# First image's attention: three key tiles of eight converted by DMA from a ring, folding with three scores of eight, VectorE's other work dealt later

## The chip, the cores and the metric

The kernel runs on one core of a Trainium2 chip. The metric is the device time of one execution in microseconds; the time of a kernel is the median of several runs. The engines are called TensorE (PE, matmuls), VectorE (DVE), ScalarE (ACT), GpSimd (POOL) and SyncE (SP); each works through its own list of instructions in order and waits on semaphores for the others. Transfers are issued from an engine's queue and carried out by the core's 16 DMA engines.

## The reference

Eight images of 512 channels and 32 x 32 = 1024 positions go through two attention layers. The first has eight heads of 64 channels, and fake-quantises q, k and v to 8 bits over the whole batch:

```python
h = group_norm(xf, gn_w, gn_b)
qkv = jnp.einsum('oc,bct->bot', qkv_w, h) + qkv_b[None, :, None]
...
q = fake_quant(q); k = fake_quant(k); v = fake_quant(v)
w = jnp.einsum('bct,bcs->bts', q * scale, k * scale)
w = jax.nn.softmax(w, axis=-1)
a = jnp.einsum('bts,bcs->bct', w, v)
a = jnp.einsum('oc,bct->bot', proj_w, a) + proj_b[None, :, None]
return xf + a
```

The second layer is a group norm and an attention with a single head of 512 channels, again with a projection and a residual. The quantisation needs the smallest and largest values of q, k and v of all images, so no attention can begin before every image's qkv is there.

## The kernel before

**Stages.** First, q, k and v of all eight images are computed and written to DRAM. Then comes the attention of the first image, with nothing of the second layer beside it, since the second layer of an image needs the whole of its first. From then on the attention of image b+1 is woven into the projection and the second layer of image b, step by step; a planner (`InOrder.planned`) with costs and due times deals the work of VectorE and ScalarE there. In the first image's attention the planner is off (`InOrder.planned` is false): `later` runs its work at once, and a hand-made list, `dealt`, takes its place.

**The attention's units.** `attention()` goes over units u = (image, head pair j, query half hf, key tile s): two halves and eight key tiles of 128 keys make 16 units for a pair, 64 for an image. For each unit,

- `scores(u)` issues two matmuls "st" (128 keys x 512 queries, for both heads of the pair) into one of two score banks, and ScalarE's exponential writes them to a float32 tile `pt` of 128 x 1024;
- `split(u)` makes two half-precision parts of it: a cast into `two[:, 0]`, and on VectorE the remainder, `two[:, 1] = pt - two[:, 0]` (a TENSOR_TENSOR, called a subtraction below);
- `over_keys` multiplies both parts with v into the bank "av", and `totals` adds up the rows into "sm" with a matmul against ones.

In the first image key tiles 3 and 7 (`plain`) aren't split: their float32 exponentials stand in a tile "aside" and go into float32 matmuls. PE's order in this stage is: scores of two units some six to eight units ahead, then av and sm of two units, and so on; the scores of tile 7 of a half stand directly ahead of the av of its tiles 0 and 1. The tiles `pt` come from a pool of four buffers, `two` from a pool of six.

**Who casts, before.** Tiles 2 and 6: GpSimd. Tile 5: VectorE (while the planner is off). Tiles 0, 1 and 4: ScalarE. The subtraction of a tile is issued straight after its cast.

**What else runs in this stage.** `fold()` multiplies the second layer's weight matrices with each other: a generator of 35 steps, mostly one float32 matmul of 128 x 512 each, with copies of the results by ScalarE and some sums by VectorE. Nine steps are taken before the attention begins; then each odd unit of the first image takes one (`next(folding, None)` in `scores`). Half-way through it issues the loads of the first image's x (2 x 1 MB, tile h), and at its end it stores four tiles (wm_d). `load_pair` fetches q and k of the next pair from DRAM 16 units ahead, and v once the second buffer `raw` is free; VectorE quantises each in two steps (`quant`, `quant2`; v has a third, `whole`, on a quarter of it for the plain tiles). `finish` ends a half: two copies by ScalarE, and after the second half the row sums go through small DMAs (`apart`, `rs_d`, `rs`) with `spread` (sum and reciprocal) and `divide` on VectorE.

`dealt` holds (unit from which it may run, name, work); `deal(u)`, called once by each `split`, runs the first entry that may run. `settle` runs all entries of a name. Before, for a pair fetched at unit u: q and k from u + 10, v's fetch from u + 10, v's steps from u + 18; spread from u + 10 and divide from u + 17 of the half's last units.

Where a unit's instructions are issued from helpers, the profile gives one line for many: L91 for VectorE's and ScalarE's, L208 for all matmuls, L1047 for GpSimd's casts. On SP, L945 are the fetches of q, k and v, L1129, L1143 and L1145 the transfers of the row sums, L1215 the loads of x, L1768 the stores of wm, L1255 the stores behind the projection.

Of the kernel before, what the change touches and what calls it, by code (L numbers as in the profile page):

```python
# [9 lines left out]
F32 = mybir.dt.float32  # L10
# [8 lines left out]
P = 128  # L19
B, C, HH, WW = 8, 512, 32, 32  # L20
T = HH * WW
CC = C // P
NT = T // P
# [35 lines left out]
def attn_pair_kernel(  # L59
# [246 lines left out]
    with ExitStack() as fast:  # L306
# [611 lines left out]
        def deal(u):  # L918
            i = next((i for i, (at, *_) in enumerate(dealt) if at <= u), None)
            if i is not None:  # L920
                dealt.pop(i)[2]()

        def settle(what):
            while True:
# [4 lines left out]
            dve.settle(what)  # L929

        ao = {}

        def load_pair(b, j, u=None):

            nm = f"{b}_{j}"
            raws = []

            def fetch(i, src):
                if (b, j, i) == (0, 0, 2):
                    raw = aop.tile([P, NH, 512], F32, tag="ao", name="raw_first").rearrange(  # L940
                        "p h n -> p (h n)"
                    )
                else:
                    raw = raw_p.tile([P, T], F32, tag="raw", name=f"raw_{nm}_{i}")
                nc.sync.dma_start(  # L945
                    raw if i < 2 else raw.rearrange("p (t d) -> p t d", t=NT), src
                )
                raws.append(raw)

            def whole(raw, _, i):  # L950
                quant2(raw.rearrange("p (t d) -> p t d", t=NT)[:, 3::4, :], vfs[j], i)

            fetch(0, q_d[b][j])
            fetch(1, k_d[b][j])
            qt = qkp.tile([P, T], BF, tag="q", name=f"q_{nm}")
            kt = qkp.tile([P, T], BF, tag="k", name=f"k_{nm}")
            vt = qkp.tile([P, NT, P], F16, tag="v", name=f"v_{nm}")
            todo = (qt, kt, vt.rearrange("p t d -> p (t d)"))

            if b == 0:  # L960
                vfs[j] = xp.tile([P, 2, 256], F32, tag="x", name=f"vf_{nm}")[:, :, 0:P]

            def quants(i):
                for step in (quant, quant2, *([whole] if i == 2 and b == 0 else [])):
                    name, work = "qk" if i < 2 else "qv", lambda step=step: step(raws[i], todo[i], i)
                    if u is None or InOrder.planned:
                        dve.later(name, 0.7, work, pe.t + 12.0, 45.0)
                    else:
                        dealt.append((u + (10 if i < 2 else 18), name, work))

            def fetch_v():
                if len(raws) == 2:
                    fetch(2, v_d[b][:, :, bass.ts(j, P)])
                quants(2)

            if (b, j) == (0, 0):
                fetch(2, v_d[b][:, :, bass.ts(j, P)])
            quants(0)
            quants(1)
            if u is None or InOrder.planned:  # L980
                dve.later("qk", 0.0, fetch_v)
            else:
                dealt.append((u + 10, "qk", fetch_v))
            return qt, kt, vt


        def attention():

# [4 lines left out]
                     for s in range(NT)]  # L993
            pairs = {}
            pairs[0, 0] = load_pair(0, 0)
            pts, parts, avs, sms, rss, ready = {}, {}, {}, {}, {}, {}
            st_free, at_hand = [0.0, 0.0], set()

            aside = l2p.tile([P, 3, NT // 2, 256], F32, tag="vsum", name="aside")
# [1 line left out]
            def scores(u):  # L1001
                b, j, hf, s = units[u]
                if hf == 0 and s == 0:
                    settle("qk")
                nm = f"{b}_{j}_{hf}"
                qt, kt, _ = pairs[b, j]
                st = pair_ps(f"st_{nm}_{s}")
                if b == 0 and u % 2 == 1:
                    next(folding, None)
                awaits(st_free[-2])  # L1010
                for i, r in enumerate(HALF):
                    mm(
                        st[:, i, :], lhsT=kt[r, bass.ts(s, P)],
                        rhs=qt[r, bass.ts(hf, 512)], start=True, stop=True,
                    )
                if u >= 4:
                    need(u - 4)
                if plain(b, s):
                    pt = aside[:, u // 4 % 3].rearrange("p (i k) n -> p i (k n)", i=2)
                else:  # L1020
                    pt = ptp.tile([P, 2, 512], F32, tag="p", name=f"pt_{nm}_{s}")
                there = act.do(
                    1.12, lambda: act.activation(pt, st, AF.Exp, scale=esc),
                    max(pe.t + 0.25, ready.get(u - 4, 0.0) + 0.1),
                )
                st_free.append(there)
                pts[u] = pt, there

            def split(u):

                b, j, hf, s = units[u]
                pt, there = pts.pop(u)
                if not InOrder.planned:
                    deal(u)
                if plain(b, s):
                    parts[u], ready[u] = pt, there
                    return
                two = partp.tile([P, 2, 2, 512], F16, tag="two", name=f"two_{b}_{j}_{hf}_{s}")
                parts[u] = two

                def rest():
                    dve.tensor_tensor(two[:, 1], pt, two[:, 0], ALU.subtract)
                    ready[u] = dve.t

                def cast(copy=act.copy):
                    at_hand.add(u)
                    copy(two[:, 0], pt)  # L1047
                    done_at = act.t if copy == act.copy else there + 1.5
                    dve.later("sum", elements(1024), rest, done_at + 0.1, 9.0)

                if s % 4 == 2:
                    cast(nc.gpsimd.tensor_copy)
                elif not InOrder.planned and s == 5:
                    cast(dve.tensor_copy)
                else:
                    act.later("cast", 1.02, cast, there, 7.0)

            def need(u):

                while u not in ready:  # L1060
                    e, name = (act, "cast") if u not in at_hand else (dve, "sum")
                    e.begin(next(i for i, c in enumerate(e.chores) if c[0] == name))
# [45 lines left out]
            def finish(b, j, hf, u):  # L1108
# [30 lines left out]
                def spread():  # L1139
# [8 lines left out]
                    if InOrder.planned:  # L1148
                        dve.later("ao", elements(1100), divide, dve.t + 7.0, 20.0)
                    else:  # L1150
                        dealt.append((u + 17, "ao", divide))

                if InOrder.planned:
                    dve.later("ao", 0.4, spread, pe.t + 5.0, 8.0)
                else:
                    dealt.append((u + 10, "ao", spread))

            for u in (0, 2, 4):
                for i in (u, u + 1):
# [542 lines left out]
        def fold():  # L1702
# [10 lines left out]

            row = l1p.tile([P, C], F32, tag="acc1", name="gn1_row")
            nc.sync.dma_start(row, vbias[2:3, :].partition_broadcast(P))
            wide = l1p.tile([P, 2, CC, 32], F32, tag="g", name="wide")
            room = l1p.tile([P, C], F32, tag="rs1", name="fold_room")

            def through(i):
# [477 lines left out]
```

## Time and profile before

| | |
|---|---|
| median of 3 runs | 2592.42 us (2591.5 to 2592.64) |
| profiled execution | 2593.63 us, span 2591.8 us |
| mean granted TensorE clock | 0.994 |
| PE, DVE, ACT, POOL busy | 2530.8, 1905.4, 1358.8, 195.6 us |
| first score matmul of the first image | 590.19 us |
| exponential of unit 3, of unit 63 | 596.24, 700.40 us |
| first matmul of the first projection | 725.53 us |
| bytes moved by DMA, mean rate | 243.09 MB, 94 GB/s |

How to read it: the span runs from the first to the last instruction. Each engine's busy time is the union of its instructions; PE's is modelled, since matmuls overlap, so gaps in it and start-to-start distances say more than its busy share. A row of the timeline is: start, duration, engine, line, operation, what is written and read, how many in a row, and in brackets how long the engine had been idle and what ended that. "aside" is the exponential of every fourth unit of the first image, and so marks the units in the timeline. A wait is written "waiting engine, tile, line <- what ended the wait: us in total, times, longest".

### The profile page before, as it was taken

How to read it: one execution, taken by the hardware profiler on the slowest of the kernel's cores; microseconds unless marked ns; L12 is line 12 of the kernel's file. 1: busy time of each engine (PE TensorE's matmuls, PEld its weight loads, DVE VectorE, ACT ScalarE, POOL GpSimd, SP SyncE). 2: the span in 40 equal slices, each digit the busy share in tenths (PEclk: the TensorE clock that was granted, in tenths of full speed). 3: DMA queues.
4: the chain of work that ended last, by engine and by line, in shares of the span. 5: the costliest groups of instructions: out<-in, count | busy, mean ns of one | idle time of the engine just before them, and what ended most of it. 6: DMA issues, size and time to landing. Idle time of an engine off the chain costs nothing.

```text
span 2591.8 us, 38710 instructions
## 1 busy us (share of the span) xinstructions
PE 2530.8 (98%) x15670; PEld 1756.9 (68%) x15670; DVE 1905.4 (74%) x2748; ACT 1358.8 (52%) x1696; POOL 195.6 (8%) x153
## 2 busy tenths in 40 slices
PE   7999999999889999999999999999999999999998
PEld 4788888873237765775677577757756775777787
DVE  6788777669867877777877787778777777775544
ACT  3222222218856675665566566747665665664121
POOL 0000000002210001000100010010001000100000
PEclk9899999999999999999999999999999999999999
DMA  4343333334311232223212331232232123212211
GB/s 168 130 146 136 114 120 121 130 124 137 115 50 54 62 115 98 62 79 111 86 58 73 121 99 58 95 112 65 79 107 99 46 79 122 83 54 82 86 37 39
DMA packets 156013, 243.09 MB, mean 94 GB/s; under 512 B 26544, under 2 KB 93104, under 8 KB 154288
## 3 DMA queue, kind: packets, MB, share of 16 engines
q1 hardware_dynamic: 125264, 182.81, 21.2%
q10 hardware_dynamic: 30560, 57.71, 6.5%
q8 instruction: 125, 2.05, 0.3%
q14 instruction: 64, 0.52, 0.1%
HBM read 153.64 MB, written 86.28 MB: 93 GB/s over the span
## 4 chain that ended last, share of the span: by engine, by line
PE 65%; DVE 3%; ACT 2%; issue 1%; DMA 1%; POOL 0%; ACTq 0%; SPq 0%; DVEq 0%
PE s L208 15%; PE o L208 14%; PE pj L208 9%; PE v2ps L208 7%; PE av L208 7%; PE g L208 6%; PE st L208 4%; PE sm L208 3%; ACT pt L91 1%; DVE acc L91 1%; DVE two L91 1%; DVE h L91 0%; DMA out_dram<-x 0%; DVE kept_u L91 0%; DVE p L91 0%
## 5 line engine op out<-in xcount | busy, mean ns | idle before, releaser
L91 ACT ACTIVATE pt<-st,esc 128x1024 f32<-128x1024 f32 x496 | 528.1, 1114 | 350.6 <-PE st L208 327.2
L91 DVE TENSOR_TENSOR two<-pt,two 128x1024 f16<-128x1024 f32 x496 | 603.9, 1233 | 131.0 <-POOL two L1047 107.3
L91 ACT CAST two<-pt 128x1024 f16<-128x1024 f32 x358 | 362.3, 1055 | 5.3 <-ACT p L91 5.1
L1047 POOL CAST two<-pt 128x1024 f16<-128x1024 f32 x128 | 173.2, 1353 | 1533.2 <-PE sm L208 768.5
L208 PE MATMUL av<-two,v 128*32 128x512 f16 x3968 | 245.8, 382 | 0.7 <-ACT ao L91 0.7
L208 PE MATMUL s<-g,h 128*128 128x256 f32 x1024 | 233.5, 381 | 0.0
L208 PE MATMUL pj<-ao,wp 128*128 128x512 f32 x512 | 223.6, 595 | 0.0
L208 PEld LDWEIGHTS s<-g,h 128*128 128x128 f32 x1024 | 193.4, 190 | 30.5 <-issue 4.3
L91 ACT ACTIVATE u_ring<-qkps,qkbt 128x512 f32<-128x512 f32 x89 | 61.0, 685 | 253.1 <-PE qkps L208 238.3
L208 PE MATMUL st<-q,k 64*128 64x512 bf16 x1024 | 166.6, 384 | 21.6 <-ACT pt L91 16.4
L208 PEld LDWEIGHTS <-v 128*32 128x32 f16 x3968 | 91.9, 96 | 134.4 <-issue 61.9
L208 PE MATMUL s<-g,sums 128*128 128x256 f32 x768 | 178.6, 382 | 0.2 <-DVE p L91 0.2
L208 PEld LDWEIGHTS pj<-ao,wp 128*128 128x128 f32 x512 | 96.3, 190 | 121.1 <-issue 110.9
L208 PE MATMUL o<-p,v 128*128 128x256 f32 x768 | 175.2, 382 | 1.0 <-DVE p L91 1.0
L208 PEld LDWEIGHTS o<-p,v 128*128 128x128 f32 x768 | 144.6, 190 | 26.8 <-issue 5.7
L208 PEld LDWEIGHTS s<-g,sums 128*128 128x128 f32 x768 | 144.8, 190 | 24.2 <-issue 4.1
L208 PEld LDWEIGHTS <-k 64*128 64x128 bf16 x1024 | 35.8, 94 | 159.8 <-issue 158.2
L208 PE MATMUL sm<-two,ones 128*32 128x512 f16 x1984 | 136.8, 381 | 0.0
L208 PE MATMUL qkps<-half,w_low 128*128 128x512 f32 x480 | 132.6, 399 | 1.9 <-DVE half L91 1.9
L208 PE MATMUL qkps<-half,w_high 128*128 128x512 f32 x480 | 134.4, 403 | 0.0
L208 PE MATMUL qkps<-half,w_mix 128*128 128x512 f32 x480 | 132.6, 399 | 0.6 <-DVE half L91 0.6
L208 PE MATMUL g<-h,wa 128*128 128x256 f32 x512 | 120.9, 385 | 1.8 <-DVE h L91 1.8
(221 smaller groups left out, 3832.1 us busy)
## 6 DMA issues: line engine op xcount, KB each, us to landing
rs<-rs_d SPq DMA_DIRECT2D x76, 256.0 KB
x<-in_x_dram SPq DMA_DIRECT2D x32, 512.0 KB
q_d<-wa SPq DMA_DIRECT2D x32, 512.0 KB
k_d<-wa SPq DMA_DIRECT2D x32, 512.0 KB
v_d<-v_ring SPq DMA_DIRECT2D x32, 512.0 KB
raw<-q_d SPq DMA_DIRECT2D x32, 512.0 KB
raw<-k_d SPq DMA_DIRECT2D x32, 512.0 KB
x_d<-h SPq DMA_DIRECT2D x64, 256.0 KB
```

The costliest lines, as they stand in the source:

```text
L91: ins = self.latest = op(*args, **kw).ins
L208: ins = nc.tensor.matmul(ps, lhsT=lhsT, rhs=rhs, **kw).ins
L1047: copy(two[:, 0], pt)
```

## The change

In the first image only (its 64 units), and in the queues around it:

- **Casting.** Tiles 0, 1 and 4 of eight are converted by a DMA that GpSimd issues, from float32 to half precision. Their exponentials stand in a ring of three places in a new tile `spare` (which takes the buffer that `wide` had, with `wide` in its first seventh), not in `pt`. Tile 6 is cast by VectorE, tiles 2 and 5 by ScalarE; GpSimd casts nothing there. ScalarE has two casts in eight units where it had three.
- **The subtraction of a converted tile** is put off (`put_off`) until the split of the third unit after it, or until `need` asks for it.
- **Folding** takes a step in units 1, 4 and 6 of eight, where it took one in every odd unit, and goes on into the second image's first units until its steps are used up.
- **Dealing.** q's steps from u + 12 and u + 13, k's from u + 14 and u + 15, v's from u + 19 to u + 21; v's fetch from u + 13, straight behind q's second step; spread from u + 12, divide from u + 20.

In the lists of instructions the matmuls keep their order but for folding's, whose last two steps (wt_f, wc_f) stand among the scores of the second image's units 4 to 7; the last copies, sums and stores of folding follow. On SP the loads of x stand behind the fetches of the third pair's v and the fourth pair's q. On VectorE the quantising of the second image's second pair moves: k's behind the first half of the projection, v's from the second half of the projection to behind the first four normalising steps of the second layer. On GpSimd 24 DMAs stand where 16 casts stood. From there on the lists are the same.

```diff
@@ deal
                 dealt.pop(i)[2]()
+                if dealt[i : i + 1] and dealt[i][2].__name__ == "fetch_v":
+                    dealt.pop(i)[2]()
...
+        CAST_BY_DMA, CAST_BY_DVE = (0, 1, 4), (6,)
...
@@ load_pair, quants
-                for step in (quant, quant2, *([whole] if i == 2 and b == 0 else [])):
+                for n, step in enumerate((quant, quant2, *([whole] if i == 2 and b == 0 else []))):
...
-                        dealt.append((u + (10 if i < 2 else 18), name, work))
+                        dealt.append((u + (12, 14, 19)[i] + n, name, work))
+                        if (i, n) == (0, 1):
+                            dealt.append((u + 13, "qk", fetch_v))
...
-            else:
-                dealt.append((u + 10, "qk", fetch_v))
             return qt, kt, vt
 
+
+        spare = l1p.tile([P, 7, CC // 2, 256], F32, tag="g", name="spare")
...
@@ scores
-                if b == 0 and u % 2 == 1:
+                if u % 8 in (1, 4, 6):
                     next(folding, None)
...
+                elif b == 0 and s in CAST_BY_DMA:
+                    at = (u // NT * len(CAST_BY_DMA) + CAST_BY_DMA.index(s)) % 3
+                    pt = spare[:, 1 + 2 * at : 3 + 2 * at].rearrange("p i k n -> p i (k n)")
...
@@ split
                 if not InOrder.planned:
+                    for v in [v for v in put_off if v < u - 2]:
+                        put_off.pop(v)()
                     deal(u)
...
+                if b == 0 and s in CAST_BY_DMA:
+                    nc.gpsimd.dma_start(two[:, 0], pt)
+                    put_off[u] = rest
+                    return
+
...
-                if s % 4 == 2:
+                if b == 0:
+                    cast(dve.tensor_copy if s in CAST_BY_DVE else act.copy)
+                elif s % 4 == 2:
                     cast(nc.gpsimd.tensor_copy)
...
@@ need
+                if u in put_off:
+                    put_off.pop(u)()
...
@@ finish
-                        dealt.append((u + 17, "ao", divide))
+                        dealt.append((u + 20, "ao", divide))
...
-                    dealt.append((u + 10, "ao", spread))
+                    dealt.append((u + 12, "ao", spread))
...
@@ fold
-            wide = l1p.tile([P, 2, CC, 32], F32, tag="g", name="wide")
+            wide = spare[:, 0].rearrange("p k n -> p (k n)")[:, 0 : 2 * CC * 32].rearrange(
+                "p (i e n) -> p i e n", i=2, e=CC
+            )
```

## The prediction

> **What bounds the kernel now.** I read the views in this order: the page, for the whole; the busy time by stage; the waits of each engine inside the stage that the diff touches; then the timeline of that stage. The page gives PE 98% of the span, so nearly everything later is TensorE's own work, and the change can only move the stage in which PE waits. That is the first image's attention. I cut it at three events of the timeline: the first score matmul (590.19 us), the exponential of unit 3 (596.24), that of unit 63 (700.40, the last "aside" one) and the first matmul of the projection (725.53).
>
> ```profile
> 590.19:596.24 6.05, 3.54 (x13) 1.00 (x13) 3.32 (x9) 6.04 (x7) 0.00 (x0) 1.00 0.43 150
> 596.24:700.40 104.16, 98.65 (x890) 31.97 (x889) 94.00 (x111) 94.66 (x106) 23.98 (x15) 0.97 0.36 118
> 700.40:725.53 25.13, 18.05 (x200) 5.86 (x197) 21.10 (x21) 22.85 (x25) 6.82 (x4) 0.93 0.22 65
> ```
>
> The columns are length, PE, weight loads, DVE, ACT, POOL, granted clock, DMA share, GB/s. In the middle stretch three engines are at 90% or more: no single one can be relieved with effect for long. It holds 60 units (one unit is one key tile of one head pair and query half): 104.16 / 7.5 = 13.9 us for eight.
>
> What one group of eight costs PE is seen where PE never waits, between two "aside" exponentials eight units apart:
>
> ```profile
> 629.16 1.11 ACT L91 ACTIVATE aside<-st,esc 128x1024 f32<-128x1024 f32 x1
> ...
> 641.38 1.13 PE L208 MATMUL fold<-wn_v 128*128 128x512 f32 x2
> 642.44 0.39 PE L208 MATMUL st<-q,k 64*128 64x512 bf16 x2
> 642.76 1.05 PE L208 MATMUL av<-two,v 128*32 128x512 f16 x16
> 642.87 1.88 POOL L1047 CAST two<-pt 128x1024 f16<-128x1024 f32 x1 [5.00 <-ACT pt L91]
> 642.87 1.11 ACT L91 ACTIVATE aside<-st,esc 128x1024 f32<-128x1024 f32 x1
> ```
>
> 642.87 - 629.16 = 13.71 us, and PE shows no idle row in it. One folding step takes 642.44 - 641.38 = 1.06 us, and there are four in eight units. So while folding lasts, PE sets the pace. The other 0.2 us per group, and PE's later waits, come from these rows (total, times, longest):
>
> ```profile
> PE st L208 <- ACT pt L91: 12.4, 13, 2.1
> ACT pt L91 <- DVE two L91: 5.7, 4, 3.6
> DVE raw L91 <- DMA raw<-v_d: 3.3, 2, 2.2
> ```
>
> A late load of v stops VectorE, which stops the exponential (no free pt buffer), which stops the next scores; the one such stall at 655 us costs PE 1.79 us of waiting and some 2 us of half-speed matmuls after it (16 av matmuls take 1.90 us instead of 1.05). After 682 us the folding steps have run out, and PE waits for ScalarE: units 55 to 63 take 700.40 - 688.19 = 12.2 us. That is ScalarE's pace with three casts in eight.
>
> **The change part by part.** ScalarE, per eight units: an exponential every 1.00 us (636.32 to 637.32), a cast 0.95, a copy 0.48. Before, 8.0 + 3 x 0.95 + 2 x 0.48 + 0.5 = 12.3; after, with two casts, 11.4. VectorE, after: six subtractions at 1.13 (three in 3.49 us at 655.53), one cast 0.65, 3.5 quantisings at 0.67 on average (the quarter-sized one 0.3), division and reciprocals 0.8, folding's share about 1.2: 11.7. It loses something else too: with POOL casting, subtractions are slower.
>
> ```profile
> L91 DVE TENSOR_TENSOR two<-pt,two 128x1024 f16<-128x1024 f32 x6 | 8.8, 1494 | 0.0
> ```
>
> 1494 ns is the mean in the group above, against 1.22 us alone; both POOL casts of a group disappear, so about 6 x 0.27 = 1.6 us of VectorE's time comes back. PE, after: 13.71 - 1.06 = 12.65, because three folding steps come in eight units and not four. Total folding work is the same; the last steps move behind unit 63. PE's 12.65 is then the largest of the three, with 10% spare on ScalarE and 7% on VectorE, the same margins at which PE ran gapless from 604 to 655 us. The middle stretch becomes 7.5 x 12.65 = 94.9 us: **-9.3**.
>
> The start: the casts of units 0 and 1 leave ScalarE ahead of exponentials 2 and 3 (2 x 0.95), but PE then waits for other things: between 0 and -1.9, I take **-1.0**. The stretch 700.40 to 725.53 is ScalarE's, with PE 18.05 of 25.13 busy: the two last folding steps fit in PE's gaps, but their two copies (wm, fold_room) go to ScalarE here: 2 x 0.48 = **+1.0** (0 to +2). The late dealing moves one pair's v quantising (two TENSOR_SCALAR) from the projection, where VectorE idles, to just behind the four normalising ones at 769.68, in front of the sums for which PE waits 3.69 us until 777.71: 2 x 0.66 = **+1.3** (0 if another wait there ends later). The k quantising goes into the first projection, where VectorE waits 1.95 us at a time: 0.
>
> The moved fetches and stores: v is now fetched right after q's second step (unit 13 of its pair, quantised from 19), about six units or 9.5 us ahead, against 648.39 to 652.98 = 4.6 us from issue to use: the stall goes. The division waits eight units behind its spread, 12.6 us; now it waits 1.4 us after seven. On SP the two 1 MB loads of x move some eight units later, near 628 us, needed at 730; one wm store stands ahead of a v fetch. SP's queue waits nowhere for long here; 0. Its bytes will collide with the new DMAs, which counts below. The ring's tile stands where "wide" stood and holds nothing longer than the tile did: 0.
>
> **The new wait.** The trace has no converting DMA and no DMA issued by POOL. Let L be the time from the end of an exponential to the landing of its half-precision copy. VectorE takes the subtractions in order, so behind a late copy stand the other subtractions, quantisings and divisions, and PE's av matmuls behind them. The room is read from a group: the exponential of tile 0 ends at 630.89 + 1.11 = 632.00, and PE reaches the av of tiles 0 and 1 at 642.76, 10.76 us later; with a group of T this is 7T/8 - 1.24, so 9.83 at T = 12.65. The two subtractions take 2.3. **A copy is hidden if L is at most 7.5 us.**
>
> What L may be: the nearest loads of the same 512 KB are
>
> ```profile
> 687.88 0.32 SPq L945 DMA_DIRECT2D raw<-k_d  x1
> ...
> 692.00 0.76 DVE L91 TENSOR_SCALAR raw<-raw,rcp 128x1024 f32<-128x1024 f32 x1 [0.37 <-DMA raw<-k_d]
> ```
>
> 4.1 us from issue to use, and 5.8 with another load in front (649.05 to 654.86). The smallest row is 2.8 us for 8 KB (713.96 to 716.78). POOL's own part is bounded by 0 and by its slowest cast, 2.99 us; nearest is its lone cast, 1.04. So L lies between 2.8 and 8.8; I take 4.5 + 1.0 = 5.5, by the 512 KB rows. There is traffic: 24 copies read 12.6 MB in 95 us on top of 118 GB/s, where the busiest slices of this stage show 348 GB/s; the queues go from 0.36 to about 0.75 full. Collisions of 1.7 us (5.8 - 4.1) are thus to be expected, and 5.5 + 1.7 = 7.2 still fits. Below nothing: ScalarE's relief alone cannot bring PE under 12.65.
>
> A rule speaks against this. VectorE's TENSOR_SCALAR rows take 0.75 us for 1024 elements, where TENSOR_TENSOR takes 1.22. The Trainium skill, "SBUF — State Buffer", section "A bandwidth-pool intuition that's wrong (but worth ruling out)", says that a GpSimd-issued DMA cannot write its descriptors while VectorE holds the shared port in a fast one-source mode, and gives 620 ns alone against 3100 ns beside a copy, free again about 115 ns after the VectorE instruction. By that page each copy could slip by a quantising and 0.1 us, an estimate of +0.9 on L, which changes no term of my sum; no run here shows it yet. "DMA: Bandwidth & Descriptors", section "Anatomy of one DMA — SWDGE (gpsimd) path", would put 2.0 us plus bytes over 436 GB/s, 3.2 us for 512 KB, an estimate by which L would be smaller than mine.
>
> **Sum.** -9.3 - 1.0 + 1.0 + 1.3 = -8.0 us. The profiled execution took 2593.63 us (span 2591.8 and 1.8 around it): 2585.6. The median of the runs is 1.2 lower, 2592.42; on its footing the forecast is **2584.4**.
>
> **Rivals.** *Partly late copies*, 0.27: L of 7.5 to 9.1 in many groups, from traffic. T = (L + 3.54) x 8/7; at L = 8.8, T = 14.1, the middle stretch 105.8, the sum +1.6 + 1.3 = +2.9: 2595.3. For it speaks the queues' load, against it that the loads of this stage land in 4 to 6 us. *Slower: the copies come last*, 0.15: POOL's generation and the converting transfer together give L = 5.8 + 2.99 + 1.7 = 10.5, VectorE stands at tile 0 in each group, PE behind it; T = 16.05, the stretch 120.4, +16.2 + 1.3 = +17.5: 2609.9. It decides from L = 8.5 (T = 13.72, sum zero) and leaves the margin of no change at 9.1. *VectorE takes over*, 0.03: POOL's issues slow its subtractions as the casts did, 11.7 + 1.6 = 13.3 per group, stretch 99.8, sum -3.1: 2589.3; that is also what remains if the relief does not reach PE.
>
> **How the numbers follow.** The forecast case has 0.55. Its best end: -9.3 - 1.9, no loss at the end, and the clock dip at 709 us gone (some 1.9 us): -13.1, 2579.3. The range runs from there to the partly late case's 2595.3, rounded outward to 2579 to 2596; outside are the slower case and little else. 0.2%, about what a measurement of this kernel can tell from no change, is 5.2 us: under 2587.2 is faster. Forecast nearly whole plus a little of the partly late case: faster 0.57; partly late and VectorE's case: same 0.28; slower 0.15.
>
> **What would show it.** Right: 60 units between the exponentials of units 3 and 63 in about 95 us; PE's wait for pt near nothing; subtractions at 1.2 us; no wait of VectorE for the copies of tiles 0, 1 and 4 above a few us; about 1.3 us more PE idle before the sums of the first image's second layer. Wrong: a row of VectorE waiting for the DMA of two of some us in each group, with PE's av behind it, or long POOL rows. The prediction falls if L passes 8.5.

## The result, and the profile after

The changed kernel took **2594.54 us** (median of 15 runs, 2592.36 to 2601.36), the kernel before, on the same chip, 2590.01 (15 runs, 2587.83 to 2594.01). The ratio is **1.0021**, with a 95% interval of 1.0014 to 1.0029: slower by 4.5 us by the medians and about 5.4 by the ratio, where 8.0 us less was forecast. The profiled execution of the changed kernel took 2593.5 us, 1.0 below its median; that of before 2593.63, which turned out to be 3.6 above its own. So the two profiles show a difference of nothing where the medians show about 5. Part of this lies ahead of the first score matmul, where no edit works: it comes at 590.19 us before and at 588.03 here. So stretches are compared below, not spans.

The windows of the changed kernel between the four events of the prediction: first score matmul, exponentials of units 3 and 63, first matmul of the projection. Columns: length, PE, weight loads, VectorE, ScalarE, GpSimd, granted clock, DMA share, GB/s.

```profile
588.03:592.18 4.15, 3.00 (x12) 0.99 (x12) 1.51 (x6) 4.14 (x4) 1.40 (x2) 1.00 0.64 224
592.18:692.23 100.05, 92.86 (x870) 28.43 (x872) 82.13 (x106) 87.30 (x97) 13.46 (x22) 0.98 0.68 164
692.23:721.03 28.80, 21.07 (x227) 7.11 (x219) 23.85 (x25) 24.13 (x28) 3.71 (x3) 0.94 0.34 112
```

The start became 1.9 us shorter and the middle stretch 4.1 (9.3 expected); the tail, from the exponential of unit 63 to the projection, grew by 3.7 (1.0 expected). ScalarE and VectorE are no longer at 90%, so the relief arrived, but PE is busy for only 92.86 of 100.05. The DMA share went from 0.36 to 0.68.

The pace of PE is the forecast one where nothing comes late. These are the "aside" exponentials of units 35, 39 and 43 with the folding between them:

```profile
647.52 1.11 ACT L91 ACTIVATE aside<-st,esc 128x1024 f32<-128x1024 f32 x1
648.02 1.13 PE L208 MATMUL fold<-wn_v 128*128 128x512 f32 x2
...
652.09 1.13 PE L208 MATMUL fold<-wn_v 128*128 128x512 f32 x2
...
654.59 1.11 ACT L91 ACTIVATE aside<-st,esc 128x1024 f32<-128x1024 f32 x1
...
655.41 1.13 PE L208 MATMUL fold<-wn_v 128*128 128x512 f32 x2
...
659.86 1.11 ACT L91 ACTIVATE aside<-st,esc 128x1024 f32<-128x1024 f32 x1
```

659.86 - 647.52 = 12.34 us for eight units with three folding steps; 12.65 was forecast. But the group from 625.17 to 642.25 took 17.08. What PE waited for from 592 to 692 us, and VectorE from 592 to 705 (total, times, longest):

```profile
PE av L208 <- DVE two L91: 5.6, 5, 1.9
PE st L208 <- ACT pt L91: 0.6, 1, 0.6
```

```profile
DVE two L91 <- DMA two<-spare: 5.4, 3, 3.6
DVE ao L91 <- DMA rs<-rs_d: 4.0, 2, 3.2
DVE raw L91 <- DMA raw<-v_d: 3.9, 2, 2.6
DVE rcs L91 <- DMA apart<-rs: 2.9, 1, 2.9
DVE ao L91 <- DMA kept_u<-rs_d: 2.3, 1, 2.3
```

In the kernel before, PE's wait for pt from 592 to 692 us was this (the 12.4 us of the prediction take in the tail):

```profile
PE st L208 <- ACT pt L91: 4.9, 4, 2.1
```

So PE's wait for pt is nearly gone in this stretch, as forecast; in its place PE waits for VectorE's subtractions, and VectorE for transfers: not only the copies, but the loads of v and of the row sums.

Then the second image. Behind the projection the changed kernel is still 4.5 us ahead (first `gps_b` matmul at 757.56, before at 762.06; 2.2 of it from ahead of the first score matmul) and loses all of it within 30 us:

```profile
763.99 1.00 DVE L91 TENSOR_TENSOR grstd_b<-grstd_b,vec 128x4 f32<-128x4 f32 x1 [3.04 <-POOL grstd_b L262]
765.02 1.92 DVE L91 TENSOR_SCALAR h<-h,gmean_b,grstd_b 128x512 f32<-128x512 f32 x4
766.85 0.75 DVE L91 TENSOR_SCALAR raw<-raw,rcp 128x1024 f32<-128x1024 f32 x1
767.63 0.75 DVE L91 TENSOR_SCALAR v<-raw,bhi 128x1024 f16<-128x1024 f32 x1
...
768.44 1.90 PE L208 MATMUL av<-two,v 128*32 128x512 f16 x16 [8.92 <-DVE v L91]
```

PE idles 8.92 us for v of the second image's second pair, whose two steps stand behind the norm, and the sixteen matmuls after it take 1.90 us instead of 1.05. In the kernel before the same matmuls show no wait:

```profile
763.95 1.05 PE L208 MATMUL av<-two,v 128*32 128x512 f16 x16
```

The windows show the clock over two stretches at or behind a wait (columns as above):

```profile
633.40:636.80 3.40, 3.40 (x20) 0.85 (x14) 3.40 (x10) 0.12 (x1) 0.00 (x0) 0.50 0.59 140
763.10:773.30 10.20, 4.86 (x40) 1.36 (x44) 7.97 (x12) 2.48 (x3) 1.86 (x2) 0.50 0.15 53
```

A wait of 1.92 us that ended at 632.89 is followed by 3.4 us at a granted clock of 0.50. About the wait of 8.92 us, which ended at 768.44, the clock is 0.50 for 10.2 us, and in the last 4.9 of them PE is working again. So a wait can cost more than its length; not every one does, since behind a wait of 1.72 us that ended at 604.83 the clock stayed at 1.00. The Trainium skill, "TensorE: Matmul & The Clock Gate", section "What's actually happening", gives a window of 3413 ns and a half clock beside the full one; both agree with the rows. It puts the half clock behind an idle window of about 3.4 us, where here an idle time of 1.92 us in one piece was followed by it.

### The profile page after: what moved, and what is told of

Its sections match the earlier page's. It is cut to its first block, busy times and chain, and to the rows that moved or that the text cites. A ratio compares the mean times of both kernels' runs of the same rounds, so it can differ in the third digit from the quotient of the medians.

```text
span 2591.7 us, 38741 instructions
## 1 busy us (share of the span) xinstructions
PE 2525.7 (97%) x15670; PEld 1752.4 (68%) x15670; DVE 1897.4 (73%) x2748; ACT 1351.1 (52%) x1688; POOL 183.5 (7%) x161
## 4 chain that ended last, share of the span: by engine, by line
PE 83%; DVE 5%; issue 3%; DMA 2%; ACT 2%; POOL 0%; SPq 0%; ACTq 0%; DVEq 0%; POOLq 0%
PE s L208 15%; PE o L208 13%; PE qkps L208 12%; PE pj L208 9%; PE av L208 7%; PE v2ps L208 7%; PE vps L208 6%; PE g L208 6%; PE st L208 4%; PE sm L208 3%; DVE two L91 1%; ACT pt L91 1%; DVE h L91 1%; DMA apart<-rs 0%; DVE kept_u L91 0%
## 5 line engine op out<-in xcount | busy, mean ns | idle before, releaser
L91 ACT ACTIVATE pt<-st,esc 128x1024 f32<-128x1024 f32 x472 | 501.8, 1114 | 348.5 <-PE st L208 329.3
L91 DVE TENSOR_TENSOR two<-pt,two 128x1024 f16<-128x1024 f32 x472 | 567.9, 1217 | 128.7 <-POOL two L1062 104.8
L91 ACT CAST two<-pt 128x1024 f16<-128x1024 f32 x350 | 354.9, 1055 | 12.9 <-PE sm L208 7.7
L1062 POOL CAST two<-pt 128x1024 f16<-128x1024 f32 x112 | 146.2, 1305 | 1456.1 <-PE sm L208 772.8
```

Source lines behind the costliest of these rows:

```text
L91: ins = self.latest = op(*args, **kw).ins
```

## The experiments

All times of a row are from its profiled execution, in us; the ratio is to the kernel before, with its 95% interval, from all runs. "Start" runs from the first score matmul to the exponential of unit 3, "to projection" is the tail. "To unit 100" runs from the first `gps_b` matmul to the exponential of the attention's unit 100, from where to unit 127 all runs are alike within 0.4 us; the last column is the sum, first score matmul to unit 100. One execution isn't the median: the profiled one lies 4.9 us below its kernel's median in e9, 3.6 below in e14, 3.5 below in e4, 3.0 above in e3 and 3.6 above in before. So a stretch can be off by some us, and only the ratio rests on all runs.

| kernel | ratio | start | units 3 to 63 | to projection | projection | to unit 100 | sum |
|---|---|---|---|---|---|---|---|
| before | 1 | 6.05 | 104.16 | 25.13 | 36.53 | 57.28 | 229.2 |
| changed | 1.0021 (1.0014-1.0029) | 4.15 | 100.05 | 28.80 | 36.53 | 61.80 | 231.3 |
| e1 v dealt | 1.0010 (1.0002-1.0019) | 4.15 | 103.22 | 28.96 | 36.53 | 56.39 | 229.3 |
| e2 x later | 1.0034 (1.0022-1.0047) | 4.15 | 105.16 | 26.53 | 36.53 | 61.88 | 234.3 |
| e3 parts by POOL | 1.0032 (1.0020-1.0044) | 4.15 | 108.72 | 26.23 | 36.54 | 62.72 | 238.4 |
| e4 all three | 1.0024 (1.0014-1.0034) | 4.14 | 105.40 | 26.51 | 36.53 | 58.29 | 230.9 |
| e6 copies alone | 1.0013 (1.0004-1.0021) | 4.15 | 112.14 | 23.28 | 37.43 | 55.77 | 232.8 |
| e7 fold alone | 0.9999 (0.9990-1.0008) | 6.05 | 100.64 | 25.09 | 36.53 | 58.80 | 227.1 |
| e5 no copies | 1.0012 (1.0003-1.0021) | 6.04 | 100.37 | 24.43 | 36.53 | 62.00 | 229.4 |
| e9 pinned | 1.0030 (1.0016-1.0043) | 4.15 | 105.68 | 27.85 | 36.63 | 57.51 | 231.8 |
| e11 pinned, early | 0.9981 (0.9971-0.9990) | 4.15 | 96.13 | 25.96 | 37.89 | 58.47 | 222.6 |
| e12 same, no copies | 0.9987 (0.9978-0.9996) | 6.05 | 97.49 | 24.19 | 38.08 | 58.14 | 224.0 |
| e13 v sooner | 0.9993 (0.9984-1.0002) | 4.14 | 100.33 | 26.91 | 38.04 | 57.78 | 227.2 |
| e14 same, no copies | 0.9975 (0.9966-0.9984) | 6.04 | 95.77 | 23.65 | 37.89 | 57.92 | 221.3 |
| e15 x later too | **0.9961** (0.9948-0.9975) | 4.15 | 93.67 | 26.62 | 38.04 | 57.66 | 220.1 |
| e16 same, no copies | 0.9978 (0.9969-0.9987) | 6.04 | 96.19 | 23.65 | 37.89 | 58.68 | 222.5 |

The first theory was that three separate places give the gain back: the late v, the loads of x among the copies (the copy of unit 17, issued at 616.50, was waited for until 624.67, with x's 2 MB issued at 619.37), and a small load behind a waiting one on SyncE's queue. The rival was that the copies cost it as such.

### e1 to e4: each loss undone alone, then together

e1. In `attention()`, `deal(u)` runs only `if not InOrder.planned`. In the changed kernel, `fetch_v` of the second image's second pair still runs before the planner takes over, so it puts the two steps of v into `dealt`, and nobody looks there again until `settle("qv")` at unit 80. The edit hands them over:

```diff
         InOrder.planned = True
+        for e in [e for e in dealt if e[1] == "qv"]:
+            dealt.remove(e)
+            dve.later("qv", 0.7, e[2], pe.t + 12.0, 45.0)
```

> One edit to the changed kernel: the two steps that quantise v of the second image's second pair, which nobody deals out once the planner has taken over, are given to the planner. Theory (three separate places give the gain back; this one gives back 4.5 us): the two steps run in the projection's gaps, before 755 us; TensorE's wait of 8.92 us for v falls to about 4 and the half-speed matmuls behind it go; ratio to the kernel before about 1.0004 (4.4 us below the changed kernel's 1.0021). Rival (the wait is the norm's, and v only came last by a hair, as the prediction priced it with 1.3 us): the wait of 8.92 goes over to another tile with at least 7.5 us left; ratio 1.0015 or more.

Measured: 1.0010, 2.8 us below the changed kernel's ratio. The steps now run in the projection, and PE's av matmuls run at full speed without a wait:

```profile
736.08 0.74 DVE L91 TENSOR_SCALAR raw<-raw,rcp 128x1024 f32<-128x1024 f32 x1
736.85 0.75 DVE L91 TENSOR_SCALAR v<-raw,bhi 128x1024 f16<-128x1024 f32 x1
```

The last stretch fell from 61.80 to 56.39, 5.4 us. The theory holds for this place. But the middle stretch, where the two kernels' instructions are the same, took 103.22 us in this execution and 100.05 in the other: with the copies this stage scatters by some us from run to run. And the rest, 0.10%, is still slower than before.

e2. The loads of x are issued at unit 64, held behind an exponential by an ordering edge:

```diff
                     load_wp(0, nc.sync.dma_start)
-                    load_x2(0, nc.sync.dma_start)
...
                 st = pair_ps(f"st_{nm}_{s}")
+                if u == 64:
+                    load_x2(0, after_exp)
```

> One edit to the changed kernel: the two 1 MB loads of x into h are issued behind the exponential of unit 64 instead of near 619 us. Theory: the copy that took over 8 us to land (unit 17) took so long only because these 2 MB went through the same 16 engines; its wait of 3.64 us, the half-clock stretch near 635 us and the group of 17.08 us go, the group falls to 12.5 to 13, and the ratio is about 1.0005 (4 us less). Rival (converting copies are late now and then whatever else runs): some group of 15 us or more stays, the landings stay at 8 us in places, ratio 1.0015 or more.

Measured: 1.0034, a miss. VectorE's wait for the copy of unit 17 was still 3.24 us (3.64 in the changed kernel) though the 2 MB were gone, so these had hardly made it late; what is left beside that copy are the copy of unit 16 and 1 MB of q and v. Other groups of 15.0 and 16.7 us appeared.

e3. In the first image the small loads of the row sums' parts are issued from GpSimd's queue instead of SyncE's:

```diff
-                    nc.sync.dma_start(
+                    (nc.gpsimd if b == 0 else nc.sync).dma_start(
                         apart[:, w, :],
```

> One edit to the changed kernel: in the first image the small loads of the reciprocals' parts (apart<-rs) are issued from GpSimd's queue instead of SyncE's, where one stood for 4 us behind a load of k that waited for its buffer. Theory: the division of the third pair comes some 3 us earlier, ScalarE's two waits for two near 699 and 703 us go, the stretch from unit 63 to the first projection matmul falls from 28.8 to about 26 us; ratio about 1.001 (2 to 3 us less). Rival (that stretch is ScalarE's own work, longer because the last fold steps and their copies moved there): still 28 or more, ratio 1.002.

Measured: the tail fell to 26.23 us as expected, but the middle stretch took 108.72 and the ratio is 1.0032. A miss for the sum.

e4 is e1, e2 and e3 together.

> The three edits together on the changed kernel. Theory (three separate losses, each undone): their sum, 4.4 + 4 + 2.5 = 11 us below the changed kernel, ratio to the kernel before about 0.9979, so faster than both kernels; every group of eight in the middle stretch between 12.3 and 14.1 us. Rival (one loss stands behind another, so that what is undone in one place is waited for in the next): at most 5 us below the changed kernel, ratio 1.0 or more.

Measured: 1.0024. The rival's number, and the first theory fell: repairs in single places didn't add up. In e4 VectorE waited 4.21 us for `kept_u`, 2.48 and 2.53 for v, 1.93 for k, none of them a copy, and besides 6.9 us in five waits for copies. So the next runs took the change apart.

### e5 to e7: one part at a time

e6 is the kernel before with the ring, the copies, their put-off subtractions and the first image's casts of the diff, and nothing else of it. e7 is the kernel before with `if u % 8 in (1, 4, 6)` in front of the folding step. e5 is the changed kernel with the casts of before: both `s in CAST_BY_DMA` branches off, and the old chain `if s % 4 == 2`.

> The kernel before with the copies by DMA alone (tiles 0, 1 and 4 through the ring, the first image's other casts as in the changed kernel); folding in every second unit and the dealing stay as they were. Theory (the copies fill the DMA engines and every load that VectorE waits for lands later; folding keeps TensorE's pace at 13.7 us for eight units): the middle stretch from unit 3 to unit 63 takes 104 to 108 us where it was 104.16, the start is 1.9 us shorter; the wait for v of the second image's second pair is not there, because that is the dealing's; ratio between 0.9995 and 1.0015. Rival (the copies cost nothing, the dealing does): middle stretch at most 103 us, ratio 0.9985 or less.

> The kernel before with folding in three of eight units instead of four; the casts stay on ScalarE, VectorE and GpSimd, the dealing as it was. Theory (TensorE's pace falls to 12.65 us for eight units, then ScalarE's 12.3 and VectorE's waits are next): middle stretch 97 to 101 us, the tail 1 to 2 us longer; ratio about 0.998 to 0.999. Rival (ScalarE and VectorE, both at 90% or more, hold the pace at 13.9 whatever folding does; only the copies could free them): middle stretch 103 or more, ratio 1.000.

> The changed kernel with the casts as they were before (no copy by DMA); folding in three of eight and the late dealing stay. Theory: the wait for v of the second pair is the dealing's, so it stays (8 to 9 us there, 4.5 us of the total); the stage before it is as in the kernel with folding alone, 3 to 5 us shorter; ratio about 1.000. If the copies are the main cost of the changed kernel, the waits of VectorE for rs, raw and apart fall from 14 to 20 us in this stage to the 9 to 11 us of the kernel before; if the dealing is, they stay.

Measured: the copies alone 1.0013, within the expected ratio, but with a middle stretch of 112.14 us, longer than either theory said; folding alone 0.9999, its middle stretch 100.64 as expected, but the later stretches took 1.5 us more, and its ratio is above the expected range; without the copies 1.0012, with PE's wait for v at 9.15 us. VectorE's waits for transfers in e5, to be set against the five rows of the changed kernel above:

```profile
DVE raw L91 <- DMA raw<-v_d: 3.2, 2, 1.6
DVE ao L91 <- DMA kept_u<-rs_d: 2.3, 1, 2.3
DVE ao L91 <- DMA rs<-rs_d: 2.0, 1, 2.0
DVE raw L91 <- DMA raw<-k_d: 0.8, 1, 0.8
DVE raw L91 <- DMA raw<-q_d: 0.5, 1, 0.5
```

8.8 us in all, against 20.0 with the copies (18.5 in the five rows, 1.5 for k and q). So both parts cost. The late dealing costs 4.7 us at v (62.00 against 57.28). With the copies VectorE waits longer for the other transfers too: from 592 to 705 us these waits are 8.8 us in e5, 9.1 in e7 and 11.5 before, all without copies, and 14.6 in the changed kernel and 18.7 in e6. But folding alone has a middle stretch as short (100.64) as the changed kernel's 100.05, so no gain of the copies shows there. What the copies take of the DMA engines is in the queue table of the changed kernel's middle stretch (packets, MB, share of the 16 engines):

```profile
q0 software_dynamic: 3441, 6.26, 34.9%
q1 hardware_dynamic: 8044, 10.04, 33.0%
```

The second theory was this. VectorE takes its queue in order, and its loads are started by its own earlier steps (raw has two buffers: v's load waits for q's second step). What counts is then how many of VectorE's instructions stand between the start of a load and its use. These are all rows of VectorE from q's step to v's first in the changed kernel:

```profile
671.40 0.75 DVE L91 TENSOR_SCALAR q<-raw,bhi 128x1024 bf16<-128x1024 f32 x1
672.06 1.22 DVE L91 TENSOR_TENSOR two<-pt,two 128x1024 f16<-128x1024 f32 x1
673.20 0.75 DVE L91 TENSOR_SCALAR k<-raw,bhi 128x1024 bf16<-128x1024 f32 x1
676.51 0.75 DVE L91 TENSOR_SCALAR raw<-raw,rcp 128x1024 f32<-128x1024 f32 x1 [2.57 <-DMA raw<-v_d]
```

v's load was issued at 672.18, behind q's step. The deals stand six units apart in the code, but in VectorE's queue only two instructions stand between, so the emitted order isn't that of the deals. (That the scheduler moved dealt steps forward and put-off subtractions back is the reading of it; e9 tests the order.)

### e9 to e16: the order of VectorE's queue

e9 is e1 with each dealt step held behind VectorE's instruction before it in program order:

```diff
             if i is not None:
+                behind = dve.latest
                 dealt.pop(i)[2]()
+                if dve.latest is not behind:
+                    tc.add_manual_dep(dve.latest, behind.name, IN_ORDER, reason="order")
```

> The changed kernel with two edits: the two steps of v that nobody deals out are given to the planner, and every dealt step is held in program order behind VectorE's instruction before it, so that the quantising of v and the division stand some 9 us behind the loads that they wait for instead of 2 to 4. Theory (VectorE takes its queue in order, and it is the short distance between a load's start and its use that makes the waits, not the landing times): VectorE's waits for raw, rs and kept_u (2.3 to 4.4 us each) fall under 1 us, the middle stretch to 95 to 98 us, the wait for v is gone; ratio about 0.9975 to 0.9985, faster than both kernels. Rival (the copies fill the DMA engines so that the loads land late at any distance, or the copies themselves come late): the middle stretch stays at 100 us or more, ratio 1.000 or more.

Measured: 1.0030, with a middle stretch of 105.68: the rival's numbers. Yet half of the mechanism showed: VectorE's waits for raw, rs and kept_u were all gone. Its waits for the copies, of which the rival spoke too, rose from 5.4 us to this (592 to 705 us):

```profile
DVE two L91 <- DMA two<-spare: 19.8, 11, 6.9
```

And PE had a new wait, four times:

```profile
610.82 0.39 PE L208 MATMUL st<-q,k 64*128 64x512 bf16 x2 [2.26 <-DVE k L91]
641.55 0.61 PE L208 MATMUL st<-q,k 64*128 64x512 bf16 x2 [4.44 <-DVE k L91]
671.08 0.39 PE L208 MATMUL st<-q,k 64*128 64x512 bf16 x2 [2.70 <-DVE k L91]
699.50 0.39 PE L208 MATMUL st<-q,k 64*128 64x512 bf16 x2 [3.68 <-DVE k L91]
```

k, dealt at units 14 and 15, was the last thing before the next pair's scores. e11 deals q, v's fetch and k four units earlier; e12 is e11 without the copies.

```diff
-                        dealt.append((u + (12, 14, 19)[i] + n, name, work))
+                        dealt.append((u + (8, 10, 19)[i] + n, name, work))
                         if (i, n) == (0, 1):
-                            dealt.append((u + 13, "qk", fetch_v))
+                            dealt.append((u + 9, "qk", fetch_v))
```

> The kernel with pinned dealing (the run before this one), and q, the fetch of v, and k dealt four units earlier (units 8 to 11 of the pair instead of 12 to 15). There the waits of VectorE for raw, rs and kept_u were all gone, but TensorE waited four times for k, 2.26, 4.44, 2.70 and 3.68 us, because k was the last thing dealt in front of the next pair's scores. Theory (the distances between a load and its use, and between VectorE's step and TensorE's need, are what counts): these four waits go, the middle stretch from unit 3 to unit 63 takes 95 to 99 us, ratio 0.9970 to 0.9990, faster than both kernels. Rival (the copies themselves are what comes late, and VectorE stands at them whatever else is dealt when): VectorE waits for two<-spare in most groups, the middle stretch takes 101 us or more, ratio 1.000 or more.

> The same dealing as in the run beside it, but without the copies by DMA: the casts as in the kernel before. ScalarE then has three casts in eight, 12.3 us, and GpSimd casts beside VectorE's subtractions. Theory: TensorE waits for ScalarE in most units, the middle stretch takes 98 to 101 us as with folding alone (100.64), the late v is gone; ratio 0.998 to 0.9995, so 1 to 3 us slower than with the copies. If the copies are what costs, this one is faster than the run beside it by 2 us or more.

Measured: 0.9981 and 0.9987, the first two kernels whose interval lies below 1. In e11 the middle stretch is 96.13; its only long group (units 23 to 31), 15.2 us, holds a wait of PE for v. VectorE still waits 13.2 us for copies in e11, in four waits. One of them, 2.95 us, ends at 613.17, and VectorE is busy from there until v's step at 622.82, so this copy may have had a part in the wait for v. The two ratios lie within each other's intervals, so nothing yet told what the copies are worth. e13 and e14 are these two with 17 for 19 in the line above, so that v's steps come two units sooner.

> The best kernel so far (pinned dealing, early) with v's steps dealt two units sooner (17 instead of 19). There TensorE waited for v three times (1.88, 0.48 and 1.99 us), two of them followed by matmuls at half speed (1.90 us for sixteen instead of 1.05). Theory (VectorE's place in its own queue, not a landing, made these waits: the load of v started some 14 us ahead): the three waits and the half-clock stretches go, the middle stretch falls from 96.13 to 93.5 to 95, the stretch from unit 63 to the projection by 2 us; 3 to 5 us less in all, ratio 0.9962 to 0.9975. Rival (VectorE's total is what is short, so the wait moves to the subtractions of the first tiles): the middle stretch stays at 96 us, ratio 0.998.

> The run beside it without the copies by DMA, the casts as in the kernel before. ScalarE holds the pace here (96.60 busy of the 100 us from 600 to 700 in the run this is built from), so v two units sooner is worth less: 0 to 2 us; middle stretch 96 to 97.5 us, ratio 0.998 to 0.999. With the copies 2 to 4 us faster than without, if the copies are worth anything once nothing else stands in VectorE's queue; if the two are equal within 1 us again, they are not.

Measured: 0.9993 and 0.9975. The waits for v went, and in e14 VectorE waited for no transfer at all. In e13 every group took 11.4 to 12.7 us, counted from unit 3, but one, of 19.8. SyncE's queue and VectorE in it:

```profile
622.18 1.06 SPq L1237 DMA_DIRECT2D h<-in_x_dram  x2
623.34 5.11 SPq L1151 DMA_DIRECT2D apart<-rs  x2
```

```profile
635.13 0.18 DVE L91 TENSOR_TENSOR rcs<-apart 128x16 f32<-128x16 f32 x1 [5.09 <-DMA apart<-rs]
```

8 KB, issued behind x's 2 MB on the same queue, stopped VectorE for 5.09 us; e15 tests whether the 2 MB were the reason. e15 and e16 are e13 and e14 with e2's edit.

> The kernel with the copies, pinned dealing and v sooner, and the two 1 MB loads of x issued behind the exponential of unit 64. In the run it is built from, every group of eight took 12.1 to 12.8 us but one of 19.8, in which VectorE waited 5.09 us for the 8 KB of apart, issued right behind these 2 MB in the same queue. Theory (one small read behind 2 MB made that stall, and the copies only filled the engines besides): the stall goes, the middle stretch falls from 100.33 to 94 to 96 us, the ratio from 0.9993 to 0.9965 to 0.9978. Rival (the copies' traffic makes some load late in every arrangement): another stall of 3 us or more takes its place, the middle stretch stays at 98 us or more, ratio 0.9985 or more.

> The same without the copies by DMA. In the run it is built from VectorE waited for no transfer at all in this stage, so moving the 2 MB changes nothing: middle stretch 95 to 97 us, ratio 0.997 to 0.998 (0.9975 before). Set against the run beside it, this one tells what the copies are worth when no load stands in their way: theory, the copies are 1 to 2 us faster (TensorE's 12.4 us for eight units against ScalarE's 12.8); rival, they are slower by 2 us or more.

Measured: **0.9961** and 0.9978. e15 is the fastest of all, 9.5 us below the kernel before (medians 2580.85 and 2590.36); its middle stretch is 93.67 us:

```profile
590.12:683.79 93.67, 90.92 (x870) 28.14 (x872) 81.43 (x104) 86.92 (x97) 12.25 (x22) 1.00 0.65 146
```

The DMA share is still 0.65, but the clock is 1.00 throughout, VectorE's wait of 5.09 us is gone, and PE's waits for VectorE's subtractions from 592 to 692 us are down from 5.6 us in the changed kernel (6.2 in e13) to this:

```profile
PE av L208 <- DVE two L91: 1.9, 4, 0.7
```

VectorE waits for the copies longer than in the changed kernel:

```profile
DVE two L91 <- DMA two<-spare: 14.0, 4, 7.3
```

7.28 us of it come ahead of its first subtraction. PE hardly shows these waits: behind three of the four it waits 0.52, 0.44 and 0.27 us, behind the other not at all. That nothing that PE needs soon stands behind them is the likely reason.

The ratios of e15 and e16 differ by 0.0017, 3.8 us by the medians. Their intervals just overlap (0.9975 and 0.9969), but only one of the 11 runs of e16 is below the longest of the 5 of e15. So with VectorE's queue in order and x's loads out of the way, the copies, with the casts that go with them, are worth about that much. With x's loads in the way the sign was the other: e13 is 4.2 us above e14. The same edit, e2, didn't help in the changed kernel (1.0034 against 1.0021).

## Why the prediction was wrong, point by point

By the profiled stretches the terms came out as -1.9 at the start (-1.0 was taken), -4.1 in the middle (-9.3), +3.7 in the tail (+1.0) and +4.5 from `gps_b` to unit 100 (+1.3): +2.2 where the sum had -8.0.

- **The term "2 x 0.66 = +1.3" for v was mis-sized.** Its place was right: behind the four normalising steps. Its price was that of VectorE's two instructions; PE's price was a wait of 8.92 us with 4.9 us of work at half clock behind it, 4.5 us net from `gps_b` to unit 100 (61.80 against 57.28). The working looked at the sums, whose wait stands later in PE's order; the av matmuls that need v stand in front of them. e1 took it away: 56.39. That nobody deals these steps out could be read in the code.
- **The middle stretch, "7.5 x 12.65 = 94.9", was the right pace, and the step to it failed:** "the same margins at which PE ran gapless from 604 to 655 us". The margins of engines say nothing about the order in a queue. VectorE was busy for 82.13 of 100.05 us and still late: it stood at transfers for 16.8 us of this stretch. e15, with the same copies and folding, another order and x's loads later, took 93.67.
- **"the stall goes" (v fetched "about six units or 9.5 us ahead") failed.** Six units of dealing were 2 us in VectorE's queue, and the wait was 2.57 us; the division's eight units still ended in waits of 2.3 and 3.2 us. e9 made the distance real, and these waits went.
- **The new wait was sized about right, and its effect was not only on the copies.** Issue to landing had a median of 4.2 us, from 2.8 to 8.1. The prediction's L, counted from the end of the exponential, was 3.2 to 8.4, within the bounds of 2.8 to 8.8 that were taken. Two of the 24 copies, units 17 and 20, were above the 7.5 that was to be hidden, and the wait for unit 17's (3.64 us) lies in the longest group, of 17.08. But the prediction let the traffic count against L alone: "Its bytes will collide with the new DMAs, which counts below". The loads and row sums were later too: VectorE's waits for others than the copies rose from 11.5 us to 14.6 from 592 to 705 us, with 5.4 for the copies themselves.
- **"SP's queue waits nowhere for long here; 0" failed.** The load of k waited for its raw buffer until 682.17, and behind it stood the row sums' small loads, whose input was ready at 678.2:

```profile
682.17 0.33 SPq L948 DMA_DIRECT2D raw<-k_d  x1
682.55 2.05 SPq L1148 DMA_DIRECT2D apart<-rs  x2
```

  From there the wait runs on to the reciprocals (2.91 us), the division (3.21) and PE at 699.81 (2.82): the tail grew by 3.7 us instead of 1.0. In e3 it was 26.23, but in e2, without that edit, 26.53, so it isn't shown that this wait alone made it longer.
- **The start** gave its full 1.9 us (1.0 was taken), and the subtractions went to 1.22 us as forecast.

The rival "partly late copies" gave nearly the right time, 2595.3, with a mechanism that is only a part of it. Its middle stretch was 105.8, and 100.05 was measured, so the nearness is luck; that the measured time lies inside the range of 2579 to 2596 is owed to this rival's end of it and says nothing for the forecast.

What stays open: how much of the scatter of the middle stretch (100.05 and 103.22 with the same instructions) is the copies' landings and how much the half-clock stretches that follow a wait; and whether early dealing without the pinning would do, which was not tried. The early orders also leave something: in e11 to e16 the projection takes 1.4 us more or so than in before, and in e11 and e15 PE waits there 1.1 and 1.2 us for a division.

## What to carry to other kernels

Price a moved step by who waits for it and what that engine does next, not by its own length: two steps of 0.75 us cost 4.5. When an engine takes its queue in order, count the instructions in its queue between a load's start and its use, in the emitted order; units of the program say nothing. An edit that adds transfers should come with a look at every other load whose user stands in the same queue, since here ScalarE was relieved by 7 us and VectorE by 12 in the middle stretch, and the gain came out (0.9961) only with the order mended and x's loads moved.

## What the runs showed of the hardware

- A copy that converts 512 KB of f32 to 256 KB of f16 within the core's memory took at least 2.8 us from GpSimd's issue to landing, 4.2 in the median, 8.1 beside another copy and the loads of q, v and x (8.8 once, in e6). The 24 of them filled the 16 engines for a share about as large as all the stage's other transfers.
- GpSimd's issue takes 0.53 us, and at times longer beside VectorE's one-source steps:

```profile
616.50 0.99 POOL L1056 DMA_DIRECT2D two<-spare  x1 [0.81 <-ACT spare L91]
```

```profile
616.62 0.74 DVE L91 TENSOR_SCALAR k<-raw,bhi 128x1024 bf16<-128x1024 f32 x1
```

  The issue ends 0.13 us after VectorE's step (617.49 and 617.36). The Trainium skill, "SBUF — State Buffer", section "A bandwidth-pool intuition that's wrong (but worth ruling out)", gives release plus some 115 ns; the row agrees. The price here was at most 0.8 us (1.30, the longest issue of the runs, in e4), less than that page's 3100 ns against 620.
- Subtractions of VectorE took 1.22 us on average from 590 to 690 us with GpSimd's issues in that stretch, where a group beside its casts took 1.49 on average.
